# One plus the exponential on ScalarE in the softplus correction of a scan's preparation

## The chip, the core and the metric

The kernel runs on one core of a Trainium2 chip. A core has five engines with an instruction queue each, worked off in order: TensorE (PE, matmuls), VectorE (DVE), ScalarE (ACT), GpSimd (POOL) and SyncE (SP, which issues DMAs here). They run beside each other[...]. The metric is the device time of one execution in microseconds. Three runs of the kernel before took 3914.04, 3920.10 and 3921.82 us.

## What is computed

Two layers, each a token mixer and a mixture of experts, on an input of 4 images with 256 channels and 32 x 32 pixels. The change lies in the mixer of the second layer, a selective scan over the pixels in four directions (rows forth and back, columns forth and back). Cut to what matters:

```python
def _selective_scan(x, A_log, D, W_delta, b_delta, W_B, W_C):
    delta = jax.nn.softplus(x @ W_delta + b_delta)
    Bm = x @ W_B
    Cm = x @ W_C
    A = -jnp.exp(A_log)
    dA = jnp.exp(delta[..., None] * A)
    dBx = (delta * x)[..., None] * Bm[:, :, None, :]
    ...
    _, h = jax.lax.associative_scan(combine, (dA, dBx), axis=1)
    y = jnp.einsum('blcn,bln->blc', h, Cm) + x * D
    return y
```

The kernel has no softplus instruction. With z = x @ W_delta + b_delta and v = exp(-|z|), it forms softplus(z) = max(z, 0) + ln(1 + v). Since 1 + v is rounded to 32 bits before the logarithm, a small v loses its last digits. A correction gives them back: v - ((1 + v) - 1) is exactly what the rounding dropped, and it is added to the logarithm.

## The kernel before

An image is held as 128 partitions x 2 channel halves (c) x 1024 pixels. The second layer's mixer has 4 images x 2 halves x 16 states (s) = 128 scans, each over 128 x 1024 elements. One scan is one `Scan` object, and the function `turn(k)` (line 2168) writes out, by hand, the order in which the instructions of neighbouring scans are put into the engines' queues: scan k's two row scans, scan k-1's column scan and sums, scan k+1's and k+2's inputs. Inside `tc.manual_schedule()` this order is the order in each queue.

What one turn puts on the engines, with the names that the profile shows:

- VectorE: `forth` (L2098, scan into h), `back` (L2105, scan into the sum in PSUM), `output` of the scan before (L2132), `come_in` (L2111, 32 elements), then a step of the next image's preparation if there is one, then `columns` (L2122, scan of the columns into h). The next turn begins with `forth` again.
- ScalarE: `column_decays` (L2065) and `products` (L2069) of the next scan; `decays` (L2073) of the next scan, into one PSUM buffer, so it waits until `back` has read the old ones; `inputs` of the next scan (L2082, a copy that turns rows into columns, after GpSimd's product L2081).
- TensorE: `columns_added` (L2127), `begin` (L2087, which clears the next sum), `third`'s sum and `back`'s sum (both L2093), `output_added` (L2136). All add into PSUM with an identity matrix.
- GpSimd: `third` (L2116), the gap (L2102), the product uu (L2081), and gathers or scatters of rows (L1921, L2016).
- SyncE: loads of the broadcast rows bb and cb (L2059, L2061).

The softplus belongs to `Prep`, the preparation of an image: normalisation, the projections, delta and dx. `Prep.steps` is a generator, and each `yield` ends a step. Images 1 to 3 are prepared beside the scans of the image before: `turn` takes one step at its start and one between `come_in` and `columns`. There `whole_rows` is True. Their projection L1866 goes to half of the PSUM sum that the next scan will use, so that `begin` (L2087) has to wait for its readers, and stands behind `columns_added` in such turns. Image 0 is prepared beside the last tiles of the first layer's experts (L1455 to L1508), with `whole_rows` False; there the order in the queues is made by the scheduler. The lines at the end of that preparation, `Lead.steps` (L1958 to L1963), make the inputs of the first scan. The tiles there share the engines with it: a Gelu on ScalarE (L1491), sums and copies on VectorE (L1466, L1500, L1506), and for completed images transposes (L1934) and copies (L1940).

In the parts of `Prep.steps` that matter, the 512-pixel pieces (`parts`, four of them) go one by one: L1866 makes z in PSUM, L1870 and L1871 make max(z, 0) and |z|, L1873 (or L1882 for all pieces at once) makes v. `lost` makes the correction of the piece before, with two VectorE instructions on 128 x 512 elements:

```python
def lost(c, cols):
    back = self.dx[:, c, cols]
    nc.vector.tensor_scalar(back, v[:, c, cols], 1.0, 1.0, ALU.add, ALU.subtract)
    nc.vector.tensor_tensor(back, v[:, c, cols], back, ALU.subtract)
```

With `whole_rows`, `lost` is called in the turn after the exponential of its piece, so four turns of each preparation have one call, the last of them without a projection. Then L1879 takes the logarithm of all pieces, in place over v, and L1890 adds the correction to it, L1891 adds the sum to max(z, 0), and L1894 and L1895 make dx and the skip term. `lost` runs 16 times in all: 4 in image 0's preparation, 12 in the turns.

Of the kernel before, what the change touches and what calls it, by code (L numbers as in the profile page):

```python
# [16 lines left out]
AF = mybir.ActivationFunctionType  # L17
ALU = mybir.AluOpType
# [48 lines left out]
def metaformer(ctx: ExitStack, tc: tile.TileContext, t: dict, out: bass.AP):  # L67
    nc = tc.nc
# [407 lines left out]
    with ExitStack() as st:  # L476
# [454 lines left out]
        def plan(first, needed, steps, places=range(PLACES)):  # L931
            todo.append([first, needed, steps, False, places])
# [674 lines left out]
    def route(b, tok, slot, space, psum, tag):  # L1607
# [22 lines left out]
        nc.vector.tensor_scalar(tok[:, :, C + 1], red, -1.0, float(E), ALU.mult, ALU.add)  # L1630
        nc.vector.tensor_copy(tok[:, :, C], goal[:, ts(b, NT)])
        yield from steps()
        nc.vector.scalar_tensor_tensor(lg1, hot1, -1e30, lg1, ALU.mult, ALU.add)
        best(m2, hot2)
# [156 lines left out]
    class Prep:  # L1791
# [7 lines left out]
        def steps(self, room, psum, tag, whole_rows):  # L1799
# [4 lines left out]
            for h in range(NHALF):  # L1804
                cols = ts(h, HALF)
# [48 lines left out]
            v = room("sp", [CT, L])  # L1854
# [2 lines left out]

            def lost(c, cols):
                back = self.dx[:, c, cols]
                nc.vector.tensor_scalar(back, v[:, c, cols], 1.0, 1.0, ALU.add, ALU.subtract)  # L1860
                nc.vector.tensor_tensor(back, v[:, c, cols], back, ALU.subtract)

            for i, (c, cols) in enumerate(parts):
                zp = psum.tile([P, HALF], F32, tag=tag, name="zp")
                for k in range(CT):
                    nc.tensor.matmul(zp, wd[:, k, ts(c, P)], xm[:, k, cols], start=(k == 0), stop=(k == CT - 1))  # L1866
                if i and whole_rows:
                    lost(*parts[i - 1])
                yield
                nc.scalar.activation(self.delta[:, c, cols], zp, AF.Relu, bias=bd[:, c : c + 1])  # L1870
                nc.scalar.activation(v[:, c, cols], zp, AF.Abs, bias=bd[:, c : c + 1])  # L1871
                if whole_rows:
                    nc.scalar.activation(v[:, c, cols], v[:, c, cols], AF.Exp, scale=-1.0)  # L1873
                yield
            log = v if whole_rows else sq
            if whole_rows:
                lost(*parts[-1])
                yield
                nc.scalar.activation(log, v, AF.Ln, bias=1.0)  # L1879
                yield  # L1880
            else:
                nc.scalar.activation(v, v, AF.Exp, scale=-1.0)  # L1882
                nc.scalar.activation(log, v, AF.Ln, bias=1.0)
                yield
                for part in parts:
                    lost(*part)
                    yield
            for c, cols in [(c, slice(0, L)) for c in range(CT)] if whole_rows else parts:
                dx = self.dx[:, c, cols]
                nc.vector.tensor_tensor(dx, dx, log[:, c, cols], ALU.add)  # L1890
                nc.vector.tensor_tensor(self.delta[:, c, cols], self.delta[:, c, cols], dx, ALU.add)  # L1891
                yield
                yield
                nc.vector.tensor_tensor(dx, self.delta[:, c, cols], xm[:, c, cols], ALU.mult)  # L1894
                nc.vector.scalar_tensor_tensor(x[b][:, c, cols], xm[:, c, cols], dsk[:, c : c + 1],  # L1895
                                               x[b][:, c, cols], ALU.mult, ALU.add)
                yield
                yield
# [69 lines left out]
    with ExitStack() as st:  # L1968
# [4 lines left out]
        def room(name, shape):  # L1973

            tag = "d" if name in ("xm", "ln_sq") else name
            return pb.tile([P, *shape], F32, tag=tag, name=name, bufs=1 if name == "sp" else None)
# [549 lines left out]
```

## Time and profile before

| what | value |
|---|---|
| median of three runs | 3920.1 us (3914.04 to 3921.82) |
| the profiled execution | 3926.21 us, its span 3924.5 us |
| mean granted TensorE clock | 0.875 |
| L1860, VectorE, 128x512 | 16 times, median 405 ns |
| L1861, VectorE, 128x512 | 16 times, median 692 ns |
| L1873, ScalarE exponential, 128x512 | 12 times, median 630 ns |
| L2098, L2105, L2122, VectorE scans, 128x1024 | 127 or more each, about 2270 ns |
| L2082, ScalarE copy, 128x1024 | 127 times, median 1982 ns |
| ScalarE's table loads at L1879, L1882, L1883 | 1283 ns each |
| the second layer's scans | 2192 to 3375 us of the span |

A timeline of the profile gives the start of an instruction in us from the start of the span, its duration in us, engine, line, operation, output and inputs, and in square brackets the idle time of the engine before it with what ended that time. A row of the table by stretches gives the stretch, its length, each engine's busy time with the number of instructions (PE, PEld, DVE, ACT, POOL), then the granted TensorE clock, the share of the DMA engines and GB/s. Durations of neighbours on one engine overlap a little (VectorE's by some 0.08 us), so steps are best measured from start to start.

### The profile page before, as it was taken

The numbers are of one execution on the slowest core, as the hardware profiler recorded it, in microseconds if no ns is written. First come the engines' busy times: TensorE is split into PE (matmuls) and PEld (weight loads), VectorE is DVE, ScalarE is ACT, GpSimd is POOL, SyncE is SP. The second block draws the span as 40 slices with busy tenths as digits, with TensorE's granted clock in tenths as the row PEclk, the third lists the DMA queues.
The fourth block names the chain that finished last, engine by engine and source line by source line (L and its number), as shares of the span: only waits on it lengthen the run. The fifth ranks groups of instructions, "written<-read, shape, count | busy, mean of one in ns | idle before, by whom it ended". The sixth has DMA issues, their size and how long they took to land. (4 is left out here: it accounts for less than half of the span.)

```text
span 3924.5 us, 49957 instructions
## 1 busy us (share of the span) xinstructions
PE 3362.2 (86%) x17139; PEld 1887.7 (48%) x17186; DVE 3047.5 (78%) x5283; ACT 2777.6 (71%) x3756; POOL 1953.5 (50%) x1772
## 2 busy tenths in 40 slices
PE   8378887888888887887688888998999989999998
PEld 5134443544354443543365433443443333688887
DVE  3589898998989898999576799999999999521113
ACT  2889999899989999998244677767767777332223
POOL 0146545484647665485444476555555656223112
PEclk8568887798777877788798999999999999999999
DMA  9400075000000000000186444334424334566666
GB/s 294 113 1 1 1 198 162 1 1 25 17 1 1 1 28 6 1 1 19 41 240 175 130 128 131 118 108 122 136 98 125 134 107 145 156 187 209 214 203 231
DMA packets 279802, 393.74 MB, mean 100 GB/s; under 512 B 80368, under 2 KB 221424, under 8 KB 279408
## 3 DMA queue, kind: packets, MB, share of 16 engines
q1 hardware_dynamic: 253824, 333.73, 27.8%
q0 software_dynamic: 21216, 53.73, 4.2%
q10 hardware_dynamic: 4496, 2.97, 0.2%
q8 instruction: 138, 2.26, 0.2%
q14 instruction: 128, 1.05, 0.1%
HBM read 280.41 MB, written 109.94 MB: 99 GB/s over the span
## 5 line engine op out<-in xcount | busy, mean ns | idle before, releaser
L829 POOL TENSOR_SCALAR dr<-s_n,last 128x1024 bf16<-128x1024 f32 x250 | 718.9, 2892 | 734.7 <-DVE state L857 401.3
L739 ACT ACTIVATE junk_a<-s_n,state 128x1024 int8<-128x1024 f32 x448 | 514.6, 1149 | 23.6 <-DVE state L863 7.4
L2116 POOL TENSOR_TENSOR da_c<-prod,come 128x1024 f32<-128x1024 f32 x128 | 257.7, 2014 | 376.8 <-DVE h L2122 323.2
L743 DVE TENSOR_SCALAR_CACHE_REDUCE junk_v<-s_n,state 128x1024 int8<-128x1024 f32 x320 | 408.7, 1277 | 8.8
L2314 ACT ACTIVATE hid<-hp,b 128x256 f32<-128x256 f32 x288 | 120.3, 470 | 333.2 <-issue 220.7
L790 DVE SCALAR_TENSOR_TENSOR w<-s_n,win 128x1024 f32<-128x1024 f32 x256 | 350.8, 1370 | 5.3
L793 DVE MAX8 win<-w 128x8 f32<-128x1024 f32 x256 | 314.5, 1229 | 8.8
L2105 DVE TENSOR_TENSOR_SCAN sum<-da,uu 128x1024 f32<-128x1024 f32 x127 | 289.7, 2281 | 31.2 <-PE sum L2087 18.0
L2127 PE MATMUL sum<-h,ident 128*128 128x512 f32 x512 | 262.6, 637 | 58.0 <-DVE h L2122 53.9
L897 ACT ACTIVATE ex<-sT 128x1024 f32<-128x1024 f32 x256 | 246.9, 1016 | 92.1 <-PE sT L889 92.1
L2323 DVE TENSOR_TENSOR ys<-yp,b2e 128x512 f32<-128x512 f32 x36 | 24.9, 692 | 361.1 <-PE yp L2320 361.1
L2081 POOL TENSOR_TENSOR uu<-dx,bb 128x1024 f32<-128x1024 f32 x127 | 304.0, 2393 | 1.6 <-DMA bb<-bc_d 1.4
L739 ACT ACTIVATE junk_a<-s_n,guess 128x1024 int8<-128x1024 f32 x256 | 294.2, 1149 | 7.2
L2098 DVE TENSOR_TENSOR_SCAN h<-da,uu 128x1024 f32<-128x1024 f32 x127 | 288.1, 2269 | 1.0 <-POOL uu L2081 1.0
L2122 DVE TENSOR_TENSOR_SCAN h<-da_c,uu 128x1024 f32<-128x1024 f32 x127 | 288.4, 2271 | 0.0
L907 PE MATMUL o_ps<-ex,vT 128*32 128x256 f32 x2048 | 236.5, 448 | 52.0 <-ACT ex L897 38.8
L2093 PE MATMUL sum<-da_c,ident 128*128 128x512 f32 x512 | 253.6, 618 | 28.3 <-POOL da_c L2116 23.1
L2065 ACT ACTIVATE da_c<-delta,a_log 128x1024 f32<-128x1024 f32 x128 | 268.1, 2094 | 5.2 <-DMA rows_y<-ys 5.2
L2325 POOL DMA_INDIRECT results<-ys,to x72 | 70.2, 974 | 399.4 <-DVE ys L2323 356.2
L2310 PE MATMUL hp<-xe,w 128*128 128x256 f32 x1152 | 258.3, 383 | 9.0 <-ACT hid L2314 5.3
L773 ACT COPY s_n<-sp 128x1024 f32<-128x1024 f32 x256 | 245.3, 1003 | 19.8 <-PE sp L765 12.0
L2093 PE MATMUL sum<-h,twice 128*128 128x512 f32 x512 | 245.5, 602 | 15.2 <-DVE sum L2105 15.2
(795 smaller groups left out, 7564.3 us busy)
## 6 DMA issues: line engine op xcount, KB each, us to landing
cb<-bc_d SPq DMA_DIRECT2D x128, 512.0 KB, 4.1
bb<-bc_d SPq DMA_DIRECT2D x127, 512.0 KB, 5.2
w<-in_w SPq DMA_DIRECT2D x36, 1024.0 KB, 5.0
w2e<-in_w SPq DMA_DIRECT2D x36, 1024.0 KB, 5.8
slots_x<-zeros SPq DMA_DIRECT2D x1, 33669.0 KB, 128.1
slots_x<-zeros SPq DMA_DIRECT2D x1, 33282.0 KB, 120.5
w<-in_w SPq DMA_DIRECT2D x72, 256.0 KB, 3.1
xs<-slots_x SPq DMA_DIRECT2D x36, 261.0 KB, 3.4
```

Of the source, the lines that this page charges most:

```text
L739: nc.scalar.activation(junk, self.row(r), AF.Sign, bias=thr, scale=-1.0, accum_out=u)
L743: nc.vector.tensor_scalar(junk, self.row(r), thr, None, ALU.is_lt, ALU.add, accum_out=u)
L790: nc.vector.scalar_tensor_tensor(w, self.row(r), self.win[:, r, 0:1], self.row(r), ALU.is_gt if r < LAST_DVE else ALU.is_ge, ALU.subtract, ...
L793: nc.vector.max(out=self.win[:, r, 1:], in_=w)
L829: ins = eng.tensor_scalar(dr, self.row(r), self.last[:, r : r + 1], None, ALU.is_lt)
L2065: nc.scalar.activation(grid(self.da_c), cols_flipped(self.prep.delta[:, self.c]), AF.Exp, scale=self.decay)
L2081: nc.gpsimd.tensor_tensor(self.uu[:, 0], self.prep.dx[:, self.c], self.bb, ALU.mult)
L2093: nc.tensor.matmul(self.sum[:, ts(h, HALF)], ident if eye is None else eye, view[:, ts(h, HW // NHALF), :], start=False, stop=last)
L2098: nc.vector.tensor_tensor_scan(rows.rearrange("p r w -> p (r w)"), self.da, self.uu[:, 0], 0.0, ALU.mult, ALU.add)
L2105: nc.vector.tensor_tensor_scan(self.sum[:, ::-1], self.da[:, ::-1], self.uu[:, 0][:, ::-1], 0.0, ALU.mult, ALU.add)
L2122: nc.vector.tensor_tensor_scan(self.hs, self.da_c, self.uu[:, 1], 0.0, ALU.mult, ALU.add)
L2127: nc.tensor.matmul(cols_flipped(self.sum[:, ts(h, HALF)]), ident, grid(self.hs)[:, :, ts(h, half)], start=False, stop=False)
```

## The change

```diff
@@ -1857,8 +1857,8 @@
             def lost(c, cols):
                 back = self.dx[:, c, cols]
-                nc.vector.tensor_scalar(back, v[:, c, cols], 1.0, 1.0, ALU.add, ALU.subtract)
-                nc.vector.tensor_tensor(back, v[:, c, cols], back, ALU.subtract)
+                nc.scalar.activation(back, v[:, c, cols], AF.Identity, bias=1.0)
+                nc.vector.scalar_tensor_tensor(back, back, 1.0, v[:, c, cols], ALU.subtract, ALU.subtract)
...
             for c, cols in [(c, slice(0, L)) for c in range(CT)] if whole_rows else parts:
                 dx = self.dx[:, c, cols]
-                nc.vector.tensor_tensor(dx, dx, log[:, c, cols], ALU.add)
+                nc.vector.tensor_tensor(dx, log[:, c, cols], dx, ALU.subtract)
                 nc.vector.tensor_tensor(self.delta[:, c, cols], self.delta[:, c, cols], dx, ALU.add)
```

1 + v is made by ScalarE (an activation with the function Identity and a bias of 1, L1860), rounded to 32 bits as it is stored in dx. VectorE then makes ((1 + v) - 1) - v in one instruction (L1861), the correction with its sign turned, and L1890 subtracts it from the logarithm instead of adding it. The calls of `lost`, their places in the steps, and all other lines stay as they are.

In the queues of the built kernel this means: 16 activations more on ScalarE and 16 instructions fewer on VectorE; GpSimd's and SyncE's queues are the same; in the turns the order of everything else is the same. In the scheduler's part, beside image 0's preparation, some instructions of VectorE, ScalarE and TensorE stand in another order. In a turn, the new activation stands on ScalarE between the copy L2082 and the next preparation step's L1870, and the new VectorE instruction stands where the two old ones stood, between L2111 and L2122.

## The prediction

> **What bounds the kernel now.** I read the page's engine shares first, then the timelines of the stretches in which the edited lines run. They run sixteen times: four in preparation 0 (2126 to 2131 us, beside the last tiles of the first mixture of experts) and twelve in preparations 1 to 3, one per scan turn, in 2291.86 to 2330.92, 2665.39 to 2702.17 and 2968.17 to 3004.95. A turn is counted from one backward scan (L2105) to the next. First the busy times of one such stretch, then one of its turns on VectorE, ScalarE and TensorE (start, duration, instruction, idle time before it):
>
> ```profile
> PE 3362.2 (86%) x17139; PEld 1887.7 (48%) x17186; DVE 3047.5 (78%) x5283; ACT 2777.6 (71%) x3756; POOL 1953.5 (50%) x1772
> ```
> ```profile
> 2665.39:2702.17 36.78, 35.32 (x83) 14.45 (x82) 35.66 (x29) 32.73 (x28) 22.08 (x16) 1.00 0.46 129
> ```
> ```profile
> 2674.68 2.30 DVE L2105 TENSOR_TENSOR_SCAN sum<-da,uu 128x1024 f32<-128x1024 f32 x1 [0.33 <-PE sum L2087]
> 2676.89 1.21 DVE L2132 TENSOR_TENSOR yc<-sum,cb 128x1024 f32<-128x1024 f32 x1
> 2678.02 0.21 DVE L2111 TENSOR_TENSOR_SCAN come<-prod,gap 128x32 f32<-128x32 f32 x1
> 2678.14 0.41 DVE L1860 TENSOR_SCALAR dx<-sp 128x512 f32<-128x512 f32 x1
> 2678.58 0.69 DVE L1861 TENSOR_TENSOR dx<-sp,dx 128x512 f32<-128x512 f32 x1
> 2679.19 2.28 DVE L2122 TENSOR_TENSOR_SCAN h<-da_c,uu 128x1024 f32<-128x1024 f32 x1
> 2681.39 2.27 DVE L2098 TENSOR_TENSOR_SCAN h<-da,uu 128x1024 f32<-128x1024 f32 x1
> 2683.99 2.30 DVE L2105 TENSOR_TENSOR_SCAN sum<-da,uu 128x1024 f32<-128x1024 f32 x1 [0.33 <-PE sum L2087]
> ```
> ```profile
> 2677.10 1.10 ACT L2073 ACTIVATE da<-delta,a_log 128x1024 f32<-128x1024 f32 x1
> 2678.14 2.01 ACT L2082 COPY uu<-uu 128x1024 f32<-128x1024 f32 x1
> 2681.55 0.69 ACT L1870 ACTIVATE delta<-sum,bd 128x512 f32<-128x512 f32 x1 [1.40 <-PE sum L1866]
> ```
> ```profile
> 2679.64 1.88 PE L1866 MATMUL sum<-xm,wd 128*128 128x512 f32 x4
> 2681.53 1.98 PE L2127 MATMUL sum<-h,ident 128*128 128x512 f32 x4
> 2683.35 0.60 PE L2087 MATMUL sum<-nought 128*128 128x512 bf16 x2
> ```
>
> The stretch of 36.78 us has TensorE busy 35.32 and VectorE 35.66: both are full. The turn lasts 9.31 us; TensorE sets its end (VectorE waits 0.33 us for L2087), and ScalarE alone has a hole, 1.40 us ahead of L1870. In the fourth turn of a preparation, which has no projection L1866, VectorE sets the end (8.9 us).
>
> **The turns of preparations 1 to 3.** Removed from VectorE: L1860 and L1861, 0.44 + 0.61 us start to start. Added: one subtraction with two tensor inputs. The nearest row is L1895, the same operation with a pointer scalar: 0.743 us, the next instruction 0.66 us after its start (2098.72 to 2099.38). A plain tensor-tensor, L1861, takes 0.69; the 0.05 between them is 0.6 us over twelve, and I take L1895. By engine time alone VectorE gains 1.05 − 0.66 = 0.39 us a turn, 4.7 us in twelve. That is what the edit could give if the operand were always there.
>
> It is not there. In the changed kernel's queues the new activation stands behind the turn's copy L2082 and ahead of the next L1870, and the new subtraction waits for ScalarE, with both scans L2122 and L2098 queued behind it. The old L1860 waited only for the exponential L1873 of the turn before, long done. The copy cannot come sooner: ScalarE's da (L2073) waits for the end of the backward scan. From the start t0 of L2105:
> - da starts at +2.42 and the copy at +3.46 (rows above), and what follows the copy starts 1.86 after it (2707.38 to 2709.24): +5.32.
> - The activation, 128x512 from and to SBUF, is nearest to L1873 (0.63 us; L1871 with a pointer and a PSUM source takes 0.68): done at +5.95.
> - VectorE was ready for it at +3.46, and stands still for 2.5 us. The subtraction starts at +6.0, L2122 at +6.66, done (2.28) at +8.94.
> - TensorE needs that result for L2127. Before, it came to L2127 at +6.85 and h was ready at +6.79; now it waits from about +7.0 to +9.0. L2087 follows 1.82 later (2681.53 to 2683.35), the next L2105 another 0.64 (2683.99): +11.46. The steady turn has da at +2.34 (2311.58 to 2313.91), so 11.4.
>
> So a turn grows from 9.3 to 11.4: **+2.1 us**. The activation itself is free on ScalarE: it fits in the hole, which grows. What else could come late stays covered: GpSimd's product uu (2.37 us) would end some 2.6 after the next t0, and the copy wants it at 3.4.
>
> By kind of turn, each against its own length before:
> - first turn of a preparation: da is late there (+2.71, ScalarE is busy until then), 11.75 − 9.3 = +2.4, three times 7.3;
> - second and third in preparations 2 and 3: 4 x 2.1 = 8.4;
> - second and third in preparation 1: 10.39 and 10.38 before, since L2087 waited there for the ScalarE copy L1940 of a completed image; this wait is now covered by the new one: 2 x 1.0 = 2.0;
> - fourth: no L2127 on the path, the two scans 2.2 apart: 6.6 + 2.2 + 2.2 = 11.0 against 8.9: 3 x 2.1 = 6.3. The logarithm L1879 overwrites what the subtraction reads, so it also waits, some 1.4 us; its reader on VectorE (L1890) comes only 3.4 us into the next turn, which covers that.
>
> Sum +24.0 us. The turns that follow have VectorE back to back (2330.92 to 2380), so nothing there wins it back, and everything later is queued behind.
>
> **The TensorE clock.** The new idle of about 2 us ahead of L2127 comes in nine turns. Of 15 gaps of 1.67 to 2.42 us before L2127 in this trace, 4 were followed by four slow matmuls, 2.99 to 3.56 us instead of 1.98, as in the first of these two rows:
>
> ```profile
> 2710.32 3.24 PE L2127 MATMUL sum<-h,ident 128*128 128x512 f32 x4 [2.26 <-DVE h L2122]
> 2731.87 1.98 PE L2127 MATMUL sum<-h,ident 128*128 128x512 f32 x4 [2.28 <-DVE h L2122]
> ```
>
> The Trainium skill (TensorE: Matmul & The Clock Gate, HAM oscillation) sets the limit for idle gaps at about 3.4 us: by it nothing is added, sum +24. By the rows, 9 x 4/15 x 1.34 us (mean excess) = +3. I take the rows; the ends are 0 and 9 x 1.34 = 12. The skill also says to keep an add on VectorE (ScalarE: Activation LUTs, Rules for kernel authors). By speed alone, L1860's 0.41 against 0.63, with the pair then in series, 0.63 + 0.66 − 1.05 = 0.24 a turn, that would be +3 over twelve; the trace puts the larger price on the place in ScalarE's queue.
>
> **Preparation 0.** Four activations more on ScalarE, three of them between the logarithm and the table load for the Gelu, which ended TensorE's first gap here; the second ended with VectorE's copy xe:
>
> ```profile
> 2131.90 2.07 PE L1489 MATMUL hp<-xe,w 128*128 128x256 f32 x4 [4.22 <-ACT hid L1491]
> 2147.56 2.07 PE L1489 MATMUL hp<-xe,w 128*128 128x256 f32 x4 [6.42 <-DVE xe L1466]
> ```
>
> The first gap grows by 3 x 0.57 = 1.7 us. But the scheduler also rebuilds VectorE's order: xe now stands ahead of a tile's last steps (L1506, L1500) and of the copy L1940, and could be done by 2142.8 instead of 2147.5. TensorE gets there about 2144.4, since one Gelu now stands behind the copy L1963 (which waits for GpSimd's product, about 2139.9, then 1.9). Net some −3 us at L1489's second gap. If that product comes as late as before (2142.08) it is −1, and if the table load's delay is carried on, +4; if the later gaps shrink too, −6. I take −3. No table load is added: 24 are in ScalarE's queue in either kernel.
>
> **Sum.** 24 + 3 − 3 = +24 us. Against the profiled execution (3926.2 us, its span 3924.5) that is 3950; the three runs' median, 3920.1, lies 6 below it, so the forecast is **3944**.
>
> **Rivals.**
> - *Only the VectorE saving counts.* If the activation were done before VectorE asks (2.5 us earlier, as it would be ahead of the copy), the turns would lose nothing: where TensorE ends them 0, in the fourth −0.4 each, and preparation 0 up to −6: about 3913. For it: ScalarE's hole. Against: the hole lies after the copy and the queue's order is fixed. It decides only if VectorE's stall is under 0.4 us. Chance 4%.
> - *TensorE turns slow in most of the nine turns.* +12 instead of +3, and slow matmuls after: 3953 to 3960. For it: the four rows. Against: in the long row of VectorE-bound turns after 2721 gaps of 2.2 us stayed fast. 12%.
> - *Part is won back*, by a preparation 0 that gains 6 and later turns with a wait of their own (the gathers in front of preparation 1's neighbours): 3930 to 3936. 12%.
> - *No difference that can be told* (within 0.2%, 7.8 us, about what the spread of the runs allows): the stall is real but a third of my size. 6%.
>
> The forecast's own case has 66%. Range 3930 to 3956: costs of −6 to +4 in preparation 0, 0 to 12 for the clock. Faster 4%, same 6%, slower 90%.
>
> **What would show it.** In the profile after: the subtraction on L1861 has about 2.5 us of VectorE idle before it, ended by ScalarE; L1860 on ScalarE starts right behind L2082; the turns measure about 11.4 (first 11.75, fourth 11.0); L2127 shows idle of about 2 us ended by L2122; L1870's hole remains. I am wrong if the turns stay near 9.3, or if L1860 stands ahead of the copy in time; if the turns are right and the total isn't, the place is 2124 to 2165 us.

## The result and the profile after

Six runs of the changed kernel have a median of 3945.82 us (3934.2 to 3952.16), six runs of the kernel before beside them 3920.8 us. The ratio is 1.0068, its 95% interval 1.005 to 1.0086: **0.7% slower**, 20 to 34 us. The profiled execution took 3949.09 us with a span of 3947.3, at a mean granted clock of 0.874 (before 0.875).

First the page's row of engine shares (busy us, share of the span, instructions) of the kernel after:

```profile
PE 3369.8 (85%) x17186; PEld 1888.4 (48%) x17186; DVE 3041.9 (77%) x5267; ACT 2787.5 (71%) x3772; POOL 1951.5 (49%) x1772
```

VectorE has 16 instructions and 5.6 us less, ScalarE 16 and 9.9 us more. Neither hints at a longer span, and TensorE's 7.6 us more come with 47 more records, since a trace misses some. The stretch of preparation 2 (columns as in the row shown of before) shows it:

```profile
2665.11:2711.68 46.57, 37.13 (x84) 15.19 (x82) 34.38 (x25) 36.82 (x33) 21.98 (x16) 0.95 0.34 102
```

It lasts 46.57 us where it was 36.78. Before, TensorE and VectorE were both full; now VectorE works 34.38 of 46.57 us and TensorE 37.13: both wait. The granted clock of this stretch is 0.95 where it was 1.00.

Now two turns of it on VectorE (start, duration, instruction, idle time before it and what ended that):

```profile
2676.81 2.30 DVE L2105 TENSOR_TENSOR_SCAN sum<-da,uu 128x1024 f32<-128x1024 f32 x1 [0.33 <-PE sum L2087]
...
2682.70 0.69 DVE L1861 SCALAR_TENSOR_TENSOR dx<-dx,sp 128x512 f32<-128x512 f32 x1 [2.35 <-ACT dx L1860]
...
2689.45 2.30 DVE L2105 TENSOR_TENSOR_SCAN sum<-da,uu 128x1024 f32<-128x1024 f32 x1 [1.68 <-PE sum L2087]
...
2695.37 0.69 DVE L1861 SCALAR_TENSOR_TENSOR dx<-dx,sp 128x512 f32<-128x512 f32 x1 [2.38 <-ACT dx L1860]
...
2700.78 2.30 DVE L2105 TENSOR_TENSOR_SCAN sum<-da,uu 128x1024 f32<-128x1024 f32 x1 [0.33 <-PE sum L2087]
```

Each subtraction is preceded by 2.35 to 2.4 us in which VectorE stands still, and the turns last 12.64 and 11.33 us instead of 9.31. What it waits for, on ScalarE in the first of the two turns:

```profile
2679.14 1.12 ACT L2073 ACTIVATE da<-delta,a_log 128x1024 f32<-128x1024 f32 x1 [1.57 <-DVE sum L2105]
2680.20 1.94 ACT L2082 COPY uu<-uu 128x1024 f32<-128x1024 f32 x1
2682.04 0.62 ACT L1860 ACTIVATE dx<-sp 128x512 f32<-128x512 f32 x1
2683.67 0.69 ACT L1870 ACTIVATE delta<-sum,bd 128x512 f32<-128x512 f32 x1 [1.00 <-PE sum L1866]
```

The activation takes 0.62 us, but it stands behind the decays and the copy, and the decays wait for L2105. On TensorE, in the same two turns:

```profile
2685.65 2.91 PE L2127 MATMUL sum<-h,ident 128*128 128x512 f32 x4 [2.02 <-DVE h L2122]
2688.36 1.06 PE L2087 MATMUL sum<-nought 128*128 128x512 bf16 x2
...
2698.32 1.99 PE L2127 MATMUL sum<-h,ident 128*128 128x512 f32 x4 [1.69 <-DVE h L2122]
```

TensorE waits 2.02 and 1.69 us for the column scan L2122, which is late with the subtraction. After the first of these waits the same four matmuls take 2.91 us instead of 1.98, and L2087 1.06 instead of 0.60: that is why the first turn is longer by 1.3 us than the second. The rows by stretches around it show what slowed them (the granted clock is the third number from the end):

```profile
2683.63:2686.57 2.94, 0.93 (x3) 0.49 (x3) 2.94 (x2) 2.87 (x4) 0.79 (x1) 1.00 0.53 216
2686.57:2689.98 3.41, 3.41 (x6) 1.32 (x5) 1.73 (x2) 2.15 (x2) 3.24 (x3) 0.50 0.00 0
2689.98:2693.00 3.02, 3.02 (x8) 1.33 (x7) 3.02 (x3) 1.21 (x2) 1.45 (x2) 1.00 0.14 46
```

For 3.41 us TensorE was granted half its clock, and most of L2127 and all of L2087 fall into that time.

**Where the time went.** I cut the spans of both profiles at the same instructions: the start of the exponential of image 0 (L1882), the L2105 with which each stretch begins, and the one with which it ends.

| part | before, us | after, us | difference |
|---|---|---|---|
| up to L1882 (code that the change doesn't touch) | 2123.94 | 2119.86 | -4.1 |
| L1882 to the first turn with a correction | 167.92 | 165.00 | -2.9 |
| the three stretches | 112.6 | 142.9 | +30.3 |
| the two parts between them | 600.5 | 599.7 | -0.8 |
| from the last stretch to the end | 919.6 | 919.9 | +0.3 |

The sum is the spans' +22.8. The first row is scatter between executions: in the kernels below L1882 starts anywhere from 2109.7 to 2128.0 us, with the same code in front of it. So a total alone cannot tell a few us, and below the stretches are compared as well as the totals.

### The profile page after: what moved, and what is told of

Its sections match the earlier page's. It is cut to its first block, busy times and chain, and to the rows that moved or that the text cites. A ratio compares the mean times of both kernels' runs of the same rounds, so it can differ in the third digit from the quotient of the medians.

```text
span 3947.3 us, 50004 instructions
## 1 busy us (share of the span) xinstructions
PE 3369.8 (85%) x17186; PEld 1888.4 (48%) x17186; DVE 3041.9 (77%) x5267; ACT 2787.5 (71%) x3772; POOL 1951.5 (49%) x1772
## 5 line engine op out<-in xcount | busy, mean ns | idle before, releaser
L2127 PE MATMUL sum<-h,ident 128*128 128x512 f32 x512 | 267.4, 647 | 80.0 <-DVE h L2122 77.1
L2105 DVE TENSOR_TENSOR_SCAN sum<-da,uu 128x1024 f32<-128x1024 f32 x127 | 289.7, 2281 | 35.5 <-PE sum L2087 28.0
L2122 DVE TENSOR_TENSOR_SCAN h<-da_c,uu 128x1024 f32<-128x1024 f32 x127 | 288.6, 2272 | 0.0
```

What stands on the lines that cost most here:

```text
L2105: nc.vector.tensor_tensor_scan(self.sum[:, ::-1], self.da[:, ::-1], self.uu[:, 0][:, ::-1], 0.0, ALU.mult, ALU.add)
L2122: nc.vector.tensor_tensor_scan(self.hs, self.da_c, self.uu[:, 1], 0.0, ALU.mult, ALU.add)
L2127: nc.tensor.matmul(cols_flipped(self.sum[:, ts(h, HALF)]), ident, grid(self.hs)[:, :, ts(h, half)], start=False, stop=False)
```

## The experiments

My theory: the operand is late by its place in ScalarE's queue. Rivals: that the three-step chain or the new instructions themselves cost the time; that image 0's preparation, whose order was rebuilt, is the cause; and for the part above the steady turn, that slow matmuls follow the longer gaps, or come by themselves. In edited kernels line numbers shift by up to eight (the subtraction is L1862, L1863 or L1864). Ratios are against the kernel before on the same chip, with 95% intervals.

### One half of the change at a time

*Turns only*: `lost` and the last step use the new form for images 1 to 3 alone.

```diff
-                nc.vector.tensor_scalar(back, v[:, c, cols], 1.0, 1.0, ALU.add, ALU.subtract)
-                nc.vector.tensor_tensor(back, v[:, c, cols], back, ALU.subtract)
+                if whole_rows:
+                    nc.scalar.activation(back, v[:, c, cols], AF.Identity, bias=1.0)
+                    nc.vector.scalar_tensor_tensor(back, back, 1.0, v[:, c, cols], ALU.subtract, ALU.subtract)
+                else:
+                    nc.vector.tensor_scalar(back, v[:, c, cols], 1.0, 1.0, ALU.add, ALU.subtract)
+                    nc.vector.tensor_tensor(back, v[:, c, cols], back, ALU.subtract)
...
```

> The change in preparations 1 to 3 alone, image 0 as before. Theory: the stretches of four turns measure 46 to 50 us as after the change, the scans begin 7 us later than after the change, time 3950 to 3953 us. Rival (image 0's gain comes from elsewhere, or the turns' cost depends on it): 3945.

*Image 0 only*: the same with `if not whole_rows`.

> The change in image 0's preparation alone, the turns as before. Theory: the scans begin 7 us earlier than before and nothing else moves, time 3912 to 3916 us. Rival (the 7 us are one execution's scatter): 3919 to 3922, scans beginning at the old place.

Turns only: 3954.78 us (3944.79 to 3959.8), ratio 1.007 (1.0051 to 1.009), stretches 142.9 us in sum, the same as after. Image 0 only: 3917.9 us, ratio 0.9989 (0.9979 to 1.0), stretches 112.6 as before, and 165.1 us from L1882 to the first turn with a correction. The whole loss lies in the twelve turns; image 0's part is a small gain, at the edge of the noise. It is not the 7 us expected: of the 7 us by which the two profiles differ at the first such turn, 4.1 lie before L1882 and are scatter.

### The same activation at another place

*Early*: in the turns, the activation goes right behind the exponential whose result it takes, a turn before VectorE asks.

```diff
             def lost(c, cols):
...
+                if not whole_rows:
+                    nc.scalar.activation(back, v[:, c, cols], AF.Identity, bias=1.0)
...
                 if whole_rows:
                     nc.scalar.activation(v[:, c, cols], v[:, c, cols], AF.Exp, scale=-1.0)
+                    nc.scalar.activation(self.dx[:, c, cols], v[:, c, cols], AF.Identity, bias=1.0)
```

> The twelve activations of the turns stand right behind the exponential of their piece, a turn before VectorE asks; image 0 as in the change. Theory (the cost is the place in ScalarE's queue): VectorE's idle ahead of the subtraction falls from 2.35 to 0 us, the turns with a projection go back to 9.3 us (in preparation 1 10.4 to 11.0, since the activation now delays the copy L1940), the fourth to 8.5, and with image 0's 7 us gained the time is 3911 to 3916 us. Rival (ScalarE's added work or the fused subtraction itself slows the turns): turns above 10.5 us, time 3935 or more.

3917.88 us (3899.5 to 3931.03), ratio 0.9979 (0.9966 to 0.9991). VectorE's timeline of this kernel in preparation 2, the subtraction between two backward scans:

```profile
2671.70 2.30 DVE L2107 TENSOR_TENSOR_SCAN sum<-da,uu 128x1024 f32<-128x1024 f32 x1 [0.51 <-PE sum L2089]
...
2675.16 0.66 DVE L1862 SCALAR_TENSOR_TENSOR dx<-dx,sp 128x512 f32<-128x512 f32 x1
...
2680.71 2.30 DVE L2107 TENSOR_TENSOR_SCAN sum<-da,uu 128x1024 f32<-128x1024 f32 x1 [0.51 <-PE sum L2089]
```

The same instructions on the same engines, with no idle time before the subtraction, and a turn of 9.01 us. So neither the instruction's nor the activation's own time makes the loss: the place does. That the turns fall to 9.0 us and not only to the 9.3 expected is explained below (*between*). This place is not free everywhere. The two middle turns of preparation 1 grew from 10.39 to 11.05, since the activation now delays the copy L1942 of a completed image, for which TensorE's L2089 waits (1.44 us).

*Between*: the activation stands between the products (L2069) and the decays (L2073) of the turn in which VectorE asks for it, behind nothing that waits for L2105. `lost` makes it for image 0 alone, as in *early*.

```diff
+    due = []
...
+                    due.append(lambda c=c, cols=cols: nc.scalar.activation(self.dx[:, c, cols], v[:, c, cols], AF.Identity, bias=1.0))
...
                 scans[k].back()
+            while due:
+                due.pop()()
             if 0 <= k + 1 < len(order):
```

> The twelve activations stand between L2069 and L2073 of the turn in which VectorE asks, ahead of the copy L2082 and away from the copy L1940. Theory: no idle ahead of the subtraction, turns 9.0 us (preparation 1: 10.4), fourth 8.4, stretches 38.3, 35.5, 35.5 us; with image 0's 3 us, 5 to 8 us under the kernel before and 1 to 2 under the variant behind the exponential. Rival (da L2073, now 0.5 us later, delays the next forward scan): turns 9.3 or more.

3915.25 us (3896.93 to 3922.13), ratio 0.9978 (0.9966 to 0.9991): **faster than before and after**, 7.5 us below the median of before beside it. ScalarE and then VectorE in one of its turns:

```profile
2673.37 0.61 ACT L1877 ACTIVATE dx<-sp 128x512 f32<-128x512 f32 x1
2673.89 1.10 ACT L2077 ACTIVATE da<-delta,a_log 128x1024 f32<-128x1024 f32 x1
```
```profile
2673.99 0.21 DVE L2115 TENSOR_TENSOR_SCAN come<-prod,gap 128x32 f32<-128x32 f32 x1
2674.12 0.67 DVE L1864 SCALAR_TENSOR_TENSOR dx<-dx,sp 128x512 f32<-128x512 f32 x1
```

The activation ends at 2673.98, 0.14 us before VectorE asks: just in time. The decays start 0.8 us later than before in the turn (3.23 against 2.42 us after L2105's start), and the copy behind them ends ahead of a hole that was there anyway. Preparation 1's middle turns stay at 10.39. And the turns are not 9.30 us but 9.01, the fourth 8.42 instead of 8.89. TensorE's timeline, to be held against the one shown of before:

```profile
2675.61 1.88 PE L1869 MATMUL sum<-xm,wd 128*128 128x512 f32 x4
2677.33 1.88 PE L2131 MATMUL sum<-h,ident 128*128 128x512 f32 x4
2679.05 0.60 PE L2091 MATMUL sum<-nought 128*128 128x512 bf16 x2
```

From the projection to the column sum it is 1.72 us here and was 1.89, from there to the clearing 1.72 and was 1.82. So before, TensorE did wait a little for VectorE's column scan in each such turn, 0.27 us that no idle bracket showed: the two engines bounded the turn together.

### What the slow matmuls hang on

The steady stall makes turns of 11.3 us; the rest of the stretches is turns in which L2127 takes 2.6 to 3.6 us. First the changed kernel once more, for how this scatters.

> The changed kernel itself, beside the others of this series. Theory: 22 to 27 us above the kernel before, the stretches of four turns 46 to 50 us, with L2127 slow in some of the nine turns that have a projection, not always in the same ones.

3941.9 us (3933.89 to 3955.85), ratio 1.0065 (1.0045 to 1.0086), stretches 46.91, 46.85 and 46.76 (after: 46.80, 46.57, 49.54). Of the nine turns with a projection 3 have a slow L2127; in after 5 had.

*Filled*: seven small matmuls that add zeros to the sum (operand `nought`) stand ahead of L2127 in the twelve turns, so that TensorE's gap is shorter. They add work and change no value.

```diff
+            def filled(self, times):
+                for _ in range(times):
+                    nc.tensor.matmul(self.sum[:, :HALF], nought, nought[:, 0:1].to_broadcast([P, HALF]),
+                                     start=False, stop=False)
...
+                if waited[0]:
+                    scans[k - 1].filled(7)
+                waited[0] = False
                 scans[k - 1].columns_added()
```

> The change, with seven matmuls that add zeros (0.22 us each, 1.5 us in all) ahead of L2127 in the twelve turns that wait. Theory (the clock falls because TensorE idles 2 us): L2127's four matmuls last 1.98 us in all nine turns, the stretches measure 45 to 46 us instead of 46.8, 46.6 and 49.5, time 3936 to 3940 us, runs closer together. Rival (the slow matmuls have another cause, or come whatever the gap): as after the change, 3943 to 3948, or longer by the matmuls.

All nine L2127 take 1.98 us, and the stretches 45.2 us each. But the total is not shorter: 3953.78 us (3942.02 to 3958.2), ratio 1.0069 (1.0051 to 1.0088). Its profile has 12 us more in the last stage, some 600 us after the last filler, where ScalarE waits three times for something remote (2.47, 4.14 and 5.51 us). The last of them:

```profile
3630.93 0.84 ACT L2325 ACTIVATE hid<-hp,b 128x256 f32<-128x256 f32 x2 [5.51 <-remote]
```

After_again, which has no filler, has one such stop of 3.41 us there; the other profiles have none, and the cause stays open. So the experiment was made again, milder.

*Filled by four*: four such matmuls, in the nine turns with a projection only (`filled(4)`, where `waited[0] and shared`).

> The change, with four zero-adding matmuls (0.88 us) ahead of L2127 in the nine turns with a projection. TensorE's gap there falls to 0.7 to 1.5 us. Theory (gaps of under 1.6 us don't bring the clock down): L2127 at 1.98 us in all nine, stretches 45 to 46 us, total 5 to 8 us under the changed kernel beside it. Rival (the run with seven was long for a reason that added matmuls bring with them): total again as long as the changed kernel or longer, with the last stage longer than 560 us.

```profile
2676.22 1.98 PE L2135 MATMUL sum<-h,ident 128*128 128x512 f32 x4 [1.55 <-DVE h L2125]
...
2687.54 1.98 PE L2135 MATMUL sum<-h,ident 128*128 128x512 f32 x4 [1.16 <-DVE h L2125]
...
2710.15 3.78 PE L2135 MATMUL sum<-h,ident 128*128 128x512 f32 x4 [3.31 <-DVE h L2125]
```

This is TensorE's timeline of that kernel: with gaps of 0.71 to 1.55 us all nine column sums are fast. In the fourth turn, which is not filled, the gap is 3.31 us and the matmuls take 3.78, off the path. The stretches are 45.2 us each again, 4.8 less than after_again in sum. The total, 3947.6 us (3942.57 to 3957.06), ratio 1.0073 (1.0057 to 1.0088), does not show it: the other parts of its profiled span are 13 us longer than after_again's, 8 of them before L1882, where the kernels are the same. So in the stretches the slow matmuls hang on the gap; that removing them shortens the kernel, no total shows.

*Twice*: the activation of the turns stands there twice, the second one idle work that makes the same values again.

```diff
+                if whole_rows:
+                    nc.scalar.activation(back, v[:, c, cols], AF.Identity, bias=1.0)
                 nc.scalar.activation(back, v[:, c, cols], AF.Identity, bias=1.0)
```

> The change with a second, idle copy of the new activation ahead of it in the twelve turns (0.54 us more in ScalarE's queue between the copy and the activation). Theory (the wait passes one to one into the turn): VectorE's idle ahead of the subtraction 2.9 us instead of 2.35, turns 0.5 us longer (11.8 where L2127 is fast), 5 to 8 us above the changed kernel beside it. Rival (the end of a turn is set by something else by now): the turns stay at 11.3, time as the changed kernel.

```profile
2695.16 1.98 PE L2129 MATMUL sum<-h,ident 128*128 128x512 f32 x4 [1.88 <-DVE h L2124]
2707.12 3.35 PE L2129 MATMUL sum<-h,ident 128*128 128x512 f32 x4 [2.69 <-DVE h L2124]
```

VectorE's idle time before the subtraction grew from 2.37 to 3.03 us, and the fast turns from 11.32 to about 11.97: a later operand is paid one to one. But the total is 3962.45 us (3956.02 to 3965.73), ratio 1.0106 (1.009 to 1.0121), 20 us above after_again, where the wait alone explains 12 x 0.65 = 7.8. In its timeline 7 of the nine column sums are slow, as the second row shows; the two fast ones follow a slow turn and have the shortest gaps, 1.88 and 2.00 us. Its stretches are 14.4 us longer than after_again's: 7.8 from the wait, the rest about what four more slow column sums cost. The two profiled spans differ by 23.5 us, and 8.5 of the other 9.1 lie before L1882, where the kernels are the same.

**Why gaps of one length go either way.** In the five profiles with slow column sums in these twelve turns (after, after_again, turns only, twice, filled by four) the granted clock falls from 1.00 to 0.50 and stays there for 3.41 us, in a few places for twice that. Within an execution the falls begin whole multiples of 3.413 us apart: in the stretches of after at 2294.04, 2686.57, 2710.46, 2986.94, 3000.60 and 3014.25 us, which is 115, 7, 81, 4 and 4 such beats. Cut at these beats, TensorE's idle time ahead of the 60 column sums of these turns sorts them without an exception: each of the 30 beats with 2.00 us or more of it ended in a fall, and none with 1.91 us or less did. So the gap of 2.41 us that ended at 2987.15 in after had 2.21 us in one beat, and its matmuls were slow; one as long, ended at 2674.35, was cut into 0.98 and 1.43, and its matmuls were fast.

### Image 0's small gain

*Three instructions for image 0*: ScalarE makes 1 + v for image 0 only, and VectorE keeps two instructions (minus one; v minus that), so that its count is as before. The turns are as before.

```diff
+                    nc.scalar.activation(back, v[:, c, cols], AF.Identity, bias=1.0)
+                    nc.vector.tensor_scalar(back, back, 1.0, None, ALU.subtract)
+                    nc.vector.tensor_tensor(back, v[:, c, cols], back, ALU.subtract)
```

> The turns as before; in image 0's preparation ScalarE makes 1 + v as in the change, and VectorE keeps two instructions a piece (the subtraction of 1, then of both), so that its work is not less than before. Counted from the start of the exponential L1882 (its line here L1887). Theory (image 0's gain comes from where the scheduler puts the copy xe and the Gelus, not from VectorE's saved work): TensorE's next L1489 after the op transposes at +20 to +22 us (before +23.6, after the change +20.5), first turn with a correction at +164 to +166 (before 167.9). Rival (the saved VectorE work is the gain): +23 or more, 167 or more.

One run each: 3910.63 us, before beside it 3912.53. L1489 in after, then in this kernel, on TensorE's timelines:

```profile
2129.37 2.07 PE L1489 MATMUL hp<-xe,w 128*128 128x256 f32 x4 [5.78 <-ACT hid L1491]
...
2140.34 1.03 PE L1489 MATMUL hp<-xe,w 128*128 128x256 f32 x4
...
2150.43 1.87 PE L1489 MATMUL hp<-xe,w 128*128 128x256 f32 x4 [3.52 <-DVE xe L1466]
```
```profile
2119.19 2.07 PE L1489 MATMUL hp<-xe,w 128*128 128x256 f32 x4 [5.78 <-ACT hid L1491]
...
2132.92 2.07 PE L1489 MATMUL hp<-xe,w 128*128 128x256 f32 x4 [5.32 <-DVE xe L1466]
```

Counted from L1882's start, the L1489 behind the transposes L1934 (the second row shown of each) comes at 20.5 us in after (2140.34 - 2119.86), at 23.25 in this kernel (2132.92 - 2109.67) and at 23.6 in before: here the copy xe was not pulled ahead, and the theory's +20 to +22 did not come. Nor did the rival's 167: the part up to the first turn with a correction is 164.7 us, as short as in after (165.0) and in image 0 only (165.1), and shorter than in before (167.9) and turns only (167.1). So the gain is owed neither to the pulled copy alone nor to VectorE's saved instruction, as far as one profile can tell: all nine profiles with the new form have 163.0 to 166.6 us here, so the nearest of the two groups lie 0.5 us apart. TensorE's idle time in the 168 us after L1882's start is 32.0 us in before and 31.3 in turns only, against 29.2, 29.1 and 28.1 in after, image 0 only and this one: its three first long gaps sum to 13.1 us (4.22 + 6.42 + 2.44) in before, in after to 11.2 (5.78 + 1.91 + 3.52), here two sum to 11.1. What these three kernels share is 1 + v on ScalarE and an order rebuilt by the scheduler; which move in it carries the gain stays open.

## Why the prediction was right, and where its terms were off

- **The stall, 2.5 us a turn, and its cause: right.** Measured 2.35 to 2.4 (2.75 in the first turn of a preparation), ended by L1860, which starts right behind L2082. From L2105's start at 2689.45 the subtraction comes at +5.92 (predicted 6.0), L2127 at +8.87 (about 9.0), the next L2105 at +11.33 (11.4). That the place costs it, and not the work, is shown by *early* and *between*.
- **The instruction: a little cheaper.** 0.69 us, not the 0.743 of the row with a pointer scalar, and 0.59 to 0.61 from start to start, not 0.66. The other end that was named, the plain tensor-tensor at 0.69, was the right row.
- **The kinds of turn: right.** First 11.7 (11.75), middle 11.3 (11.4), fourth 10.9 (11.0), preparation 1's middle turns 11.3 instead of 10.4. The stretches without a slow L2127, those of *filled by four*, sum to 135.7 us, +23.1 over before; predicted +24.0. The first turn of preparation 1, 13.33 us with its own slow matmul, is in the next term. One reading was off: VectorE is not quite back to back behind the first stretch, but waits 2.81 us for TensorE at 2358.51 (1.07 us after the change). The parts between the stretches won back 0.8 us, less than scatter.
- **The clock: the right step, half the size.** +3 was said, from 4 slow of 15 gaps at 1.34 us each. The stretches of after, after_again and turns only lie 7.2, 4.8 and 7.2 us above 135.7: 5, 3 and 5 slow of nine, at some 1.5 us each. The share was mis-sized: the 15 gaps of the trace before include a long VectorE-bound row that stayed fast. Its turns of 10.1 to 10.2 us are nearly three beats of 3.41, so that each gap was cut at about the same place (from 2721 us on, at most 1.78, 1.80 and 1.85 us in one beat); turns of 11.3 us and longer shift against the beat. The rival with most of the nine turns slow was half right: five of nine in after, but 7 us and not 12. The trace was still the better guide: by the Trainium skill's limit for idle gaps (TensorE: Matmul & The Clock Gate, HAM oscillation; about 3.4 us) the term would be 0, with no gap over 2.41 us in the turns counted.
- **Image 0, -3: right in size, right in its reason for one step only.** The mean of the nine profiles with its new form is 2.6 us below that of the two with the old. The L1489 behind the transposes came at +20.48 (worked out: +20.46), and the first gap grew by 1.56 us (1.7). But a wait of 1.91 us ahead of it was not foreseen, nor one of 3.52 us behind it where before had 2.44, and *three instructions* gains as much without that step.
- **The sum.** 23.1 + 6 - 2.6 = +26.5 us, against the measured +20 to +34 and the predicted +24. That 3945.82 lies so near the 3944 said is in part luck: the stall was put 1 us too large and the clock 3 too small.
- **The rival that the saving alone counts** needed the activation done before VectorE asks. *Between* makes just that, and lands 7.5 us below before, where the rival had 7. That is near by luck: it had 1.2 us from the turns and up to 6 from image 0, and the stretches gave 3.1 and image 0 some 2.6. Its working for the turns was off in one point: turns that TensorE ends were put at no gain, and each gave 0.29 us, since VectorE bounded them too. VectorE's time alone would make 5.5 us (12 x 0.46, with the measured 0.59); preparation 1's first three turns, the middle two bound by the copy of a completed image, give nothing.

## What to carry to other kernels

When work moves to an engine with room, ask where in that engine's queue it will stand and what the instruction ahead of it waits for: here 0.62 us of free work cost 2.1 us a turn behind the decays and the copy, and nothing ahead of them. The busy times cannot tell these two apart; the start of the consumer against the end of the producer, counted from one fixed point of the turn, can. And before calling an engine off the path, look at gaps from start to start: a partner that waits 0.27 us in each turn may show no idle time at all.

## What the runs showed of the hardware

- **Gaps of about 2 us in a dense stream of matmuls can halve TensorE's clock.** In these turns no column sum behind a gap of at most 1.55 us was slow (18 in *filled* and *filled by four*); behind gaps of 1.57 to 2.41 us 13 of 27 were (after, after_again, turns only), and behind 1.88 to 3.08 us 7 of 9 (*twice*). What decided was the idle time within one beat of 3.41 us: 2.00 us or more brought a fall to 0.50 for the next 3.41 us, 1.91 or less did not. In the nine turns with a projection a fall cost some 1.5 us. This is read from these turns alone: in before, three falls (at 2601.69, 2891.82 and 2902.06 us) end beats with only 0.20 to 0.67 us of idle time, in which TensorE worked on sixteen matmuls of one column (L1820). So the beat counts more than idle time, and what it counts these runs do not settle.
- **The same instructions ahead of L1882 take times 18 us apart** between executions (L1882 starts at 2109.7 to 2128.0 us), so effects of a few us had to be read between fixed instructions.
